# Two transformer layers in one program: feed forward's root on VectorE, layer 1's shifts by one product, two heads joined while leaving the bank, and a new table of ranks

## The chip, the core and the metric

The kernel runs on one core of one Trainium2 chip. The metric is the device time in microseconds (us) of one execution. PE is the matrix engine (TensorE), DVE is VectorE, ACT is ScalarE, POOL is GpSimd, and SP is the engine whose queue issues most DMAs. Each engine takes its instructions strictly in the order in which they were put into its queue, and waits at an instruction whose inputs are not there.

## The reference

Two layers over x of 4 batches x 512 tokens x 128 channels, 16 heads of 8 channels, windows of 64. Each layer adds attention times a gate:

```python
xn = layernorm(x)
s = L0_attn(xn)                 # masked window of 64 keys, 16 query and 4 value heads, fitness per head
g = silu(L0_ffn(xn))            # 8 experts; each token goes to one expert: gelu(x@w1+b1)@w2+b2, times 2
x = x + s * g
xn = layernorm(x)
s = L1_attn(xn)                 # below
g = silu(L1_ffn(xn))            # 8 experts, one per token: relu(x@w1+b1)@w2+b2
x = x + s * g

def L1_attn(h):
    y = layernorm(h, ln1)
    q, k, v = y @ wq + bq, y @ wk + bk, y @ wv + bv
    ctx = windows of 64 tokens, stepped by 32, softmax(q k^T / sqrt(8)) v,
          neighbouring windows blended with linear weights
    out = ctx @ wproj + bproj + h
    f = gelu(layernorm(out, ln2) @ w1 + b1) @ w2 + b2     # the feed forward
    return f + out
```

## The kernel before

**Tiles.** Attention of either layer goes through 16 tiles of 128 tokens (batch b, tile t). Each tile is a pipeline of steps: scores one way (s0, s1) only to get each query's largest score, then scores the other way (e0, e1) with the shift by that largest score added on PE, exp on ACT, the product with the values (ov0, ov1), a copy from the bank to SBUF (osb), PE transposes back to token order (o1), and the division by the row sum. Heads are kept as 4 groups (g) of 4 (j); in layer 1 a tile has two shifted sets of windows (par 0 and 1) and two blocks of 64 keys (w 0 and 1).

**Experts.** Both expert layers sort the 2048 tokens by expert into 23 blocks of 128 (`route`, from line 492). For every block POOL gathers its tokens (xb, line 609), SP fetches the weights (lines 615-630), PE does xt (a transpose), h and y, and POOL scatters the result to DRAM (yt, line 666). Each scatter follows the scatter before it. When all 23 are there, `gates` (line 672) loads the result back.

**Layer 1's shift** (in `queries1`, lines 1286-1303): DVE takes the maxima mx (L1290), `split` writes them as three bf16 terms into `shb` (L468-472), PE transposes `shb` (tr_sh), ACT copies it out (shd, L1298), and DVE multiplies it by four masks (sh4, L1301, 128 x 256 each). In `scores_k1` 16 products of 12 rows x 64 columns per tile add it to the scores.

**Layer 1's outputs** (`values1`, `outs1`): the two banks of a tile (w 0, 1) are copied whole, 128 x 512 each, by ACT or DVE, whichever the planner has free (`copied`, L344). PE transposes eight blocks of 128 x 128, a bank for each par; only the half of the columns that belongs to a head is read from them. DVE takes the reciprocals (L1380, once for each par), multiplies by the blend (L1382) and scales (L1386).

**Layer 1's feed forward** (`feed1`, eight halves named by batch and u, 0 or 2): pr (projection), sum and statistics on DVE, then 1/sqrt(variance + eps): DVE adds eps (`rsqrt`, L392) and POOL raises to the power -1/2 (L393). DVE normalizes (hn, L428), PE transposes (tr_hn), then f, gelu and fy. `rsqrt_many` (L395-408) is the same root by shifts and three Newton steps, 13 instructions on DVE; layer 0's queries and keys use it.

**What sets the order.** All steps are generators ("threads"). `run` (line 357) plays a small planner while the program is built: it keeps a time for PE (`now["T"]`), slots for DVE, ACT, POOL and SP, and takes next the thread that can start first; a tie goes to the smaller rank from the table at the end (one number for each thread and batch). `spent(cost, steps, events)` books a step: PE's cost times `pace()`, then the listed engine times. The order of each engine's queue comes from these booked times (`settle`). Where the planner sees PE waiting, `awake` puts products of ones of 128 x 512 in front of the next step (fillers), one for each 0.3 us.

Of the kernel before, what the change touches and what calls it, by code (L numbers as in the profile page):

```python
# [9 lines left out]
F32 = mybir.dt.float32  # L10
BF16 = mybir.dt.bfloat16
# [46 lines left out]
def two_layers(  # L58
# [43 lines left out]
    def bank(name):  # L102
        return awake(ps_m.tile([P, 512], F32, tag="m", name=name))
# [167 lines left out]
    def after(event):  # L271

        return None, max(0.0, at[event] - max(now["T"], now["-"]))
# [53 lines left out]
    def pace():  # L327
        return 1.8 if now["T"] < 70.0 else 1.12
# [66 lines left out]
    def rsqrt_many(dst, src, scale, eps):  # L395

        n = dst.shape[1]
        x = small.tile([P, n], F32, tag="rq_x", name=f"rq_x_{dst.tensor.name}", bufs=1)
        nc.vector.tensor_scalar(x, src, scale, eps, ALU.mult, ALU.add)
        y = small.tile([P, n], F32, tag="rq_y", name=f"rq_y_{dst.tensor.name}", bufs=1)  # L400
        nc.vector.tensor_single_scalar(y.bitcast(I32), x.bitcast(I32), 1, ALU.logical_shift_right)
        nc.vector.tensor_scalar(y.bitcast(I32), y.bitcast(I32), -1.0, float(0x5F3759DF), ALU.mult, ALU.add)
        nc.vector.tensor_scalar_mul(x, x, -0.5)
        z = small.tile([P, n], F32, tag="rq_z", name=f"rq_z_{dst.tensor.name}", bufs=1)
        for i in range(3):
            nc.vector.tensor_tensor(z, y, y, ALU.mult)
            nc.vector.tensor_tensor(z, z, x, ALU.mult)
            nc.vector.scalar_tensor_tensor(dst if i == 2 else y, z, 1.5, y, ALU.add, ALU.mult)
# [83 lines left out]
    def route(mask, n):  # L492
# [7 lines left out]
        with tc.high_priority():  # L500
# [53 lines left out]
            spent(0.35, [("D", 1.0)] * 7, [("rows", n)])  # L554
            in_places = []
            for q in range(2):
                in_place = att_p.tile([P, NTOK // 2, P], BF16, tag="osb0", name=f"in_place_{n}_{q}")
                i = q * NTOK // 2
                for u in range(NTOK // 2):
                    nc.vector.tensor_single_scalar(in_place[:, u], place_at, placef[:, i + u : i + u + 1], ALU.is_equal)  # L560
                in_places.append(in_place)
                spent(0, [after(("rows", n)), ("D", 1.2)], [("places", n, q)])
# [351 lines left out]
    shbs1 = prepared("shb1_", 2, [P, 2, G, 32], BF16)  # L914
    later.close()
# [288 lines left out]
    def project1():  # L1204

        for b in range(B):
            yield "-", [("xn1", b), ("s1", (b - 1) * NT - 1)]
# [30 lines left out]
    def queries1():  # L1238


        for i in range(NTILE):
# [52 lines left out]
            split(shb, mx, f"1_{b}_{t}")  # L1294
            spent(1.15, [("D", 2.45), ("D", 1.0)], [("s1", i), ("shb", i)], scores=1)
            yield "M", [("shb", i), ("e1", i - 2)]
            shd = att_p.tile([P, 2 * P], BF16, tag="shd1", name=f"shd1_{b}_{t}")
            nc.scalar.copy(shd, transposed16(shb.rearrange("p a g r -> p a (g r)"), 2, f"sh1_{b}_{t}"))  # L1298
            sh4 = att_p.tile([P, 2, J, P], BF16, tag="sh4_1", name=f"sh4_1_{b}_{t}")
            for j in range(J):  # L1300
                nc.vector.tensor_scalar_mul(sh4[:, :, j], shd.rearrange("p (a f) -> p a f", a=2), smask[:, j : j + 1])  # L1301
            asked1[i] = q4, sh4, v
            spent(0.13, [("A", 0.4), ("D", 1.2)], [("sh1", i)])

    def scores_k1():
        for i in range(NTILE):
# [9 lines left out]
            for par in range(2):  # L1316
# [8 lines left out]
                for w in range(2):  # L1325
                    for g in range(G):
                        r = slice(32 * g, 32 * g + NS * J)
                        mm(
                            ps[g // 2][w * KB : (w + 1) * KB, g % 2, par], ones16[r, 0:KB],
                            sh4[r, par, :, w * KB : (w + 1) * KB], start=False, stop=True,  # L1330
                        )
# [3 lines left out]
            spent(1.45, [("Ae", 1.03), ("Ae", 1.03)], [("e1", i)], scores=2)  # L1335

    def values1():
        for i in range(NTILE):
# [15 lines left out]
            osb = att_p.tile([P, 2, J, 2, KB], F32, tag="osb1", name=f"osb1_{b}_{t}", bufs=1)  # L1354
            ovs1[i] = osb
            for w, event in enumerate(("ov1", "ov1b")):
                copied(
                    osb[:, :, :, w].rearrange("p a j f -> p (a j) f"), ov[w].rearrange("p a c d f -> p (a c d) f"),
                    0.1 if w else 1.35, [(event, i)],
                )  # L1360

    def outs1():
        for i in range(NTILE):
# [4 lines left out]
            got = []  # L1368
            rec = small.tile([P, 2, 2, 2 * G], F32, tag="rec1", name=f"rec1_{b}_{t}")
            att = att_p.tile([P, 2, D], F32, tag="att1", name=f"att1_{b}_{t}", bufs=2)  # L1370
            for par in range(2):
                tp = bank(f"o1_{b}_{t}_{par}")
                for j in range(J):
                    turn(tp[:, j * P : (j + 1) * P], osb[:, par, j].rearrange("p w f -> p (w f)"), ident)

                tp = tp.rearrange("p (c h e) -> p c h e", c=2, e=32)
                skewed = [list(d) for d in tp.ap]
                skewed[1][0] += VC
                got.append(bass.AP(tensor=tp.tensor, offset=tp.offset, ap=skewed[0:3] + [[skewed[3][0], VC]]))
                nc.vector.reciprocal(rec[:, par], got[par][:, :, :, HD])  # L1380
                spent(0.5, [("D", 0.22)])
# [9 lines left out]
            spent(0, [("D", 0.85)], [("o1", i)], banks=2)  # L1391
# [21 lines left out]
    def feed1():  # L1413


        for b in range(B):
            for u in range(0, NT, 2):
# [16 lines left out]
                rsqrt(rs, mv[:, :, 1], LN_EPS)  # L1434
                centred(hn[:, two], res[:, two], mv, rs)
                spent(1.0, [("D", 0.7), ("D", 0.7), ("G", 1.0), ("D", 0.7)], [("pr", b, u)])
# [34 lines left out]
    def combine1():  # L1471
# [13 lines left out]
        (moe_h(0, gelu), 0, 59, 111, 16),  # L1485
        (scores_k1(), 87, 25, 32, 64),
        (project1(), 92, 81, 14, 102),
        (queries1(), 107, 26, 4, 78),
        (combine0(), 19, 20, 21, 22),
        (moe_load(0, xd0, w1_0, C_B1_0), 109, 42, 85, 68),  # L1490
        (moe_load_2(0, w2_0, b2_0), 18, 74, 23, 2),
        (gates(0, yt0), 56, 5, 6, 8),
        (values1(), 66, 112, 86, 55),
        (prepare0(), 31, 65, 95, 50),
        (moe_load(1, xd1, w1_1, C_B1_1), 35, 84, 34, 38),
        (moe_load_2(1, w2_1, b2_1), 101, 118, 37, 44),
        (scores_q(), 70, 36, 104, 94),
        (moe_x(0), 73, 93, 43, 96),
        (contexts1(), 11, 12, 54, 13),
        (project0(), 88, 106, 63, 62),  # L1500
        (moe_y(0, yt0), 117, 82, 90, 41),
        (moe_x(1), 67, 40, 46, 72),
        (gates(1, yt1), 103, 49, 114, 10),
        (values0(), 48, 15, 115, 124),
        (scores_k(), 33, 1, 58, 97),
        (route(mask0, 0), 45, 100, 24, 76),
        (fitness0(), 79, 61, 91, 69),
        (combine1(), 29, 30, 39, 99),
        (route(mask1, 1), 51, 83, 9, 75),
        (moe_y(1, yt1), 121, 71, 113, 127),  # L1510
        (outs0(), 47, 57, 125, 119),
        (masked0(), 7, 52, 53, 17),
        (moe_h(1, relu), 60, 3, 122, 105),
        (prepare1(), 27, 108, 28, 80),
        (outs1(), 120, 110, 116, 89),
        (feed1(), 126, 98, 123, 77),
# [45 lines left out]
```

## Time and profile before

| | us |
|---|---|
| median of 4 runs | 494.67 |
| lowest, highest | 493.94, 497.28 |
| the profiled execution's own time | 495.05 |
| span of its profile | 493.4 |
| mean granted TensorE clock | 0.925 of full speed |

The span runs from the first to the last recorded piece of work; the profiled execution's own time is 1.65 us longer. "Busy" is the time in which an engine had an instruction in work. In the groups, a line reads: source line, engine, operation, output<-input, partitions x elements, count, then busy time, mean length of one in ns, and the engine's idle time before them with what ended it. In the waits: who waited for whom, us in total, times, the longest. In the timeline: start, length, engine, line, operation, and in brackets the engine's idle time just before.

### The profile page before, as it was taken

The numbers are of one execution on the slowest core, as the hardware profiler recorded it, in microseconds if no ns is written. First come the engines' busy times: TensorE is split into PE (matmuls) and PEld (weight loads), VectorE is DVE, ScalarE is ACT, GpSimd is POOL, SyncE is SP. The second block draws the span as 40 slices with busy tenths as digits, with TensorE's granted clock in tenths as the row PEclk, the third lists the DMA queues.
The fourth block names the chain that finished last, engine by engine and source line by source line (L and its number), as shares of the span: only waits on it lengthen the run. The fifth ranks groups of instructions, "written<-read, shape, count | busy, mean of one in ns | idle before, by whom it ended". The sixth has DMA issues, their size and how long they took to land.

```text
span 493.4 us, 14720 instructions
## 1 busy us (share of the span) xinstructions
PE 414.8 (84%) x5663; PEld 293.1 (59%) x5663; DVE 339.4 (69%) x1013; ACT 261.3 (53%) x513; POOL 178.8 (36%) x251
## 2 busy tenths in 40 slices
PE   5877797999798687599999896878999993789985
PEld 2643564676565452355565574646879883678863
DVE  6799998553856978858774584884676660675565
ACT  1422665798477534374645655444666452346622
POOL 5751445536432222242410304136352336632311
PEclk9687699999999977679999998998999998799999
DMA  5404454867243010200000000061453673442032
GB/s 171 130 1 129 119 148 108 223 155 201 52 116 96 12 54 23 64 1 3 3 23 3 3 1 23 2 153 27 131 151 94 188 205 93 126 116 76 19 107 65
DMA packets 61894, 42.12 MB, mean 85 GB/s; under 512 B 11328, under 2 KB 54208, under 8 KB 61824
## 3 DMA queue, kind: packets, MB, share of 16 engines
q1 hardware_dynamic: 58464, 34.85, 25.7%
q0 software_dynamic: 2944, 6.04, 4.7%
q8 instruction: 45, 0.74, 0.6%
q10 hardware_dynamic: 416, 0.29, 0.2%
q14 instruction: 25, 0.20, 0.1%
HBM read 34.99 MB, written 6.16 MB: 83 GB/s over the span
## 4 chain that ended last, share of the span: by engine, by line
PE 47%; DVE 27%; issue 9%; ACT 6%; DMA 5%; POOL 4%; SPq 1%; POOLq 0%; ACTq 0%; DVEq 0%
PE e L83 8%; PE s L83 6%; PE h L83 5%; PE y L83 4%; PE ov L83 4%; DVE mx L1009 3%; DVE mx L1290 3%; PE fy L83 3%; PE f L83 2%; PE qkv L83 2%; DMA xb<-xd,tokens_at 2%; ACT th L1017 2%; DMA wb<-in_w 1%; PE v L83 1%; DVE sm L1009 1%
## 5 line engine op out<-in xcount | busy, mean ns | idle before, releaser
L666 POOL DMA_INDIRECT yt<-yb,put_at x46 | 46.1, 1002 | 103.4 <-DMA yt<-yb,put_at 18.5
L609 POOL DMA_INDIRECT xb<-xd,tokens_at x46 | 45.3, 984 | 51.5 <-DVE tokens_at L586 17.1
L83 PE MATMUL h<-xbT,wb 128*128 128x128 f32 x368 | 51.4, 292 | 2.2 <-ACT xbT L344 1.3
L83 PE MATMUL y<-wb,hb 128*128 128x128 f32 x368 | 49.3, 283 | 3.5 <-ACT hb L696 3.2
L83 PEld LDWEIGHTS h<-xbT,wb 128*128 128x128 f32 x368 | 46.6, 203 | 8.5 <-issue 3.3
L83 PEld LDWEIGHTS y<-wb,hb 128*128 128x128 f32 x368 | 45.6, 197 | 7.0 <-ACT hb L696 3.9
L83 PE MATMUL e<-q,kd 32*64 32x256 f32 (+1 forms) x864 | 43.7, 444 | 0.4 <-ACT pt L1106 0.4
L1017 ACT ACTIVATE th<-s 128x768 f32<-128x768 f32 x32 | 26.0, 813 | 29.7 <-DVE mx L1009 29.1
L1333 ACT ACTIVATE pt<-e 128x1024 f32<-128x1024 f32 x32 | 31.0, 1021 | 19.7 <-PE e L83 19.7
L1290 DVE TENSOR_REDUCE mx<-s 128x16 f32<-128x1024 f32 x32 | 37.6, 1218 | 4.7 <-PE s L83 4.6
L83 PE MATMUL s<-k,qd 32*32 32x384 f32 (+1 forms) x1024 | 37.2, 484 | 2.6 <-ACT pt L1333 2.3
L83 PEld LDWEIGHTS <-ones 12*64 12x64 bf16 (+2 forms) x439 | 21.4, 105 | 28.1 <-issue 20.0
L1106 ACT ACTIVATE pt<-e 128x1024 f32<-128x1024 f32 x32 | 31.0, 1021 | 13.0 <-PE e L83 13.0
L1009 DVE TENSOR_REDUCE mx<-s 128x8 f32<-128x768 f32 x32 | 29.3, 950 | 11.8 <-PE s L83 11.8
L344 ACT COPY osb<-ov 128x512 f32<-128x512 f32 x33 | 18.5, 587 | 27.1 <-PE ov L83 21.7
L696 ACT ACTIVATE hb<-h,bb 128x128 f32<-128x128 f32 x92 | 26.4, 381 | 10.4 <-PE h L83 9.8
L1009 DVE TENSOR_REDUCE sm<-th 128x8 f32<-128x768 f32 x32 | 30.0, 948 | 1.3 <-ACT th L1017 1.0
L83 PE MATMUL ov<-pt,va 64*32 64x128 f32 (+1 forms) x896 | 28.9, 290 | 0.4 <-DVE ctx L344 0.2
L83 PEld LDWEIGHTS e<-q,kd 32*64 32x64 f32 x864 | 19.0, 136 | 11.2 <-issue 6.0
L1251 POOL TENSOR_TENSOR q<-qd,jmask 128x640 f32<-128x640 f32 x16 | 19.9, 1257 | 14.8 <-PE e L83 13.5
L704 ACT ACTIVATE hb<-h,bb 128x128 f32<-128x128 f32 x56 | 15.8, 375 | 14.5 <-PE h L83 11.9
L83 PE MATMUL e<-sh,ones 12*64 12x256 bf16 (+1 forms) x320 | 20.5, 305 | 3.6 <-DVE sh L1301 3.6
(287 smaller groups left out, 899.3 us busy)
## 6 DMA issues: line engine op xcount, KB each, us to landing
wb<-in_w SPq DMA_DIRECT2D x92, 256.0 KB
bb<-in_b SPq DMA_DIRECT2D x46, 64.0 KB
acc<-yt SPq DMA_DIRECT2D x8, 256.0 KB
xd<-ln_a SPq DMA_DIRECT2D x4, 256.0 KB
xd<-xr SPq DMA_DIRECT2D x4, 256.0 KB
out<-acc SPq DMA_DIRECT2D x8, 128.0 KB
x<-in_x SPq DMA_DIRECT2D x3, 256.0 KB
bb<-in_cols SPq DMA_DIRECT2D x46, 2.0 KB
```

Source lines behind the costliest of these rows:

```text
L83: ins = nc.tensor.matmul(*args, **kw)
L344: (nc.scalar.copy if e == "A" else nc.vector.tensor_copy)(dst, src)
L609: nc.gpsimd.indirect_dma_start(out=xb, out_offset=None, in_=xd, in_offset=bass.IndirectOffsetOnAxis(ap=tokens_at[:, k : k + 1], axis=0),)
L666: nc.gpsimd.indirect_dma_start(out=yt, out_offset=bass.IndirectOffsetOnAxis(ap=routed[n][0][:, k : k + 1], axis=0), in_=y, in_offset=None,)
L696: nc.scalar.activation(h[:, c, :], src[:, c * P : (c + 1) * P], AF.Gelu, bias=bias[:, c : c + 1])
L704: nc.scalar.activation(dst, src_c, AF.Relu, bias=b)
L1009: nc.vector.tensor_reduce(dst[:, t, 8 * gg : 8 * gg + 8].rearrange("p (u j) -> p u j", u=2), src.rearrange("p u (j f) -> p u j f", j=J), A ...
L1017: nc.scalar.activation(th, ps[gg], AF.Tanh, scale=0.5 * SCALE)
L1106: nc.scalar.activation(pt[:, 2 * gg : 2 * gg + 2], ps[gg], AF.Exp)
L1251: engine.tensor_tensor(dst, src[:, None, o : o + TW].to_broadcast([P, J, TW]), jmask[:, :, None].to_broadcast([P, J, TW]), ALU.mult,)
L1290: nc.vector.tensor_reduce(mx.rearrange("p a g j -> p g a j")[:, 2 * gg : 2 * gg + 2], ps[gg], AX.X, ALU.max, negate=True,)
L1333: nc.scalar.activation(pt[:, 2 * gg : 2 * gg + 2], ps[gg], AF.Exp, scale=SCALE)
```

## The change

1. `feed1` calls `rsqrt_many` instead of `rsqrt`: POOL's power is gone, and 13 small DVE instructions of two columns take its place. `rsqrt_many` takes one size of scratch tile for all its callers.
2. Layer 1's shift: `split` writes a compact tile (`terms`), and one DVE product with a mask (`own`) writes it into `shb` once for each of the two key blocks. Two products with `fold` (128 x 64) take the place of the two transposes; ACT's copy and the four mask products have half the columns. In `scores_k1` 8 products of 32 rows x 128 columns (`lane`) take the place of 16.
3. Layer 1's outputs: each bank leaves by one ACT instruction (two heads, scaled by `pick`) and one DVE instruction that adds the other two. `osb` has half the size and two buffers. Four transposes instead of eight, in one bank, and one reciprocal.
4. Five small constants (`own`, `fold`, `lane`, `smask1`, `pick`) are made by ten DVE instructions.
5. The planner's numbers: `pace` is 1.45 and 1.08 for 1.8 and 1.12, the routing's DVE steps are booked shorter, and all 128 ranks are others. So most steps of both layers stand elsewhere in every queue.

```diff
     def pace():
-        return 1.8 if now["T"] < 70.0 else 1.12
+        return 1.45 if now["T"] < 70.0 else 1.08
...
-            spent(0.35, [("D", 1.0)] * 7, [("rows", n)])
+            spent(0.35, [("D", 0.47)] * 7, [("rows", n)])
...
+            if b == 0:
+                yield "-", [("mask", 0)]
+                half = small.tile([P, 2, 2], F32, tag="half", name="half", bufs=1)
+                nc.vector.tensor_reduce(half[:, 0], ident.rearrange("p (w q) -> p w q", w=2), AX.X, ALU.add)
+                nc.vector.tensor_copy(own, half[:, 0])
+                nc.vector.tensor_tensor(fold, ident16[:, 0:KB], ident16[:, KB:P], ALU.add)
...
             shb = shbs1[i % 2]
-            split(shb, mx, f"1_{b}_{t}")
+            terms = small.tile([P, 2, G, NS * J], BF16, tag="terms", name=f"terms_{b}_{t}", bufs=1)
+            split(terms, mx, f"1_{b}_{t}")
+            nc.vector.tensor_tensor(
+                shb.rearrange("p a g (c r) -> p (a g) c r", c=2)[:, :, :, 0 : NS * J],
+                terms.rearrange("p a g r -> p (a g) r")[:, :, None].to_broadcast([P, 2 * G, 2, NS * J]),
+                own[:, None, :, None].to_broadcast([P, 2 * G, 2, NS * J]), ALU.mult,
+            )
...
-            shd = att_p.tile([P, 2 * P], BF16, tag="shd1", name=f"shd1_{b}_{t}")
-            nc.scalar.copy(shd, transposed16(shb.rearrange("p a g r -> p a (g r)"), 2, f"sh1_{b}_{t}"))
-            sh4 = att_p.tile([P, 2, J, P], BF16, tag="sh4_1", name=f"sh4_1_{b}_{t}")
+            for par in range(2):
+                mm(ps[:, par], shb[:, par].rearrange("p g r -> p (g r)"), fold, start=True, stop=True)
+            nc.scalar.copy(shd, ps)
+            sh4 = att_p.tile([P, 2, J, KB], BF16, tag="sh4_1", name=f"sh4_1_{b}_{t}")
...
-                for w in range(2):
-                    for g in range(G):
-                        r = slice(32 * g, 32 * g + NS * J)
-                        mm(
-                            ps[g // 2][w * KB : (w + 1) * KB, g % 2, par], ones16[r, 0:KB],
-                            sh4[r, par, :, w * KB : (w + 1) * KB], start=False, stop=True,
-                        )
+                for g in range(G):
+                    r = slice(32 * g, 32 * g + 32)
+                    mm(ps[g // 2][:, g % 2, par], lane[r], sh4[r, par], start=False, stop=True)
...
             for w, event in enumerate(("ov1", "ov1b")):
-                copied(
-                    osb[:, :, :, w].rearrange("p a j f -> p (a j) f"), ov[w].rearrange("p a c d f -> p (a c d) f"),
-                    0.1 if w else 1.35, [(event, i)],
+                nc.scalar.activation(osb[:, :, :, w], ov[w][:, :, 0], AF.Copy, scale=pick[:, 0:1])
+                nc.vector.scalar_tensor_tensor(
+                    osb[:, :, :, w], ov[w][:, :, 1], pick[:, 1:2], osb[:, :, :, w], ALU.mult, ALU.add
                 )
...
-                for j in range(J):
-                    turn(tp[:, j * P : (j + 1) * P], osb[:, par, j].rearrange("p w f -> p (w f)"), ident)
+                for d in range(2):
+                    o = (2 * par + d) * P
+                    turn(tp[:, o : o + P], osb[:, par, d].rearrange("p w f -> p (w f)"), ident)
...
-                rsqrt(rs, mv[:, :, 1], LN_EPS)
+                rsqrt_many(rs, mv[:, :, 1], 1.0, LN_EPS)
                 centred(hn[:, two], res[:, two], mv, rs)
-                spent(1.0, [("D", 0.7), ("D", 0.7), ("G", 1.0), ("D", 0.7)], [("pr", b, u)])
+                spent(1.0, [("D", 0.7), ("D", 0.75), ("D", 0.75), ("D", 0.75)], [("pr", b, u)])
...
-        (moe_h(0, gelu), 0, 59, 111, 16),
-        (scores_k1(), 87, 25, 32, 64),
+        (moe_h(0, gelu), 72, 107, 99, 117),
+        (scores_k1(), 13, 11, 102, 80),
...
```

## The prediction

> **What bounds the kernel now.** I read the page first, for each engine's share and its course over time.
>
> ```profile
> span 493.4 us, 14720 instructions
> PE 414.8 (84%) x5663; PEld 293.1 (59%) x5663; DVE 339.4 (69%) x1013; ACT 261.3 (53%) x513; POOL 178.8 (36%) x251
> PE   5877797999798687599999896878999993789985
> DVE  6799998553856978858774584884676660675565
> ```
>
> PE is the bound in most slices. DVE is it in the first fifth: between 23 and 75 us it is busy for 49.6 of 52. PE has 78.6 us of idle time, so next I asked the waits which of it is long.
>
> ```profile
> PE tr_hn L88 <- DVE hn L428: 12.5, 3, 10.4
> DVE hn L428 <- POOL rs_d L393: 20.6, 8, 13.3
> POOL yt L666 <- DMA yt<-yb,put_at: 18.5, 6, 4.1
> ```
>
> One wait of 10.4 us stands out, of PE on the feed forward's hn, and DVE's wait on POOL's power behind it is longer still (13.3). The timeline shows its place:
>
> ```profile
> 407.38 0.16 DVE L392 TENSOR_SCALAR rs_d<-mv_d 128x2 f32<-128x2 f32 x1
> ...
> 416.21 1.00 POOL L666 DMA_INDIRECT yt<-yb,put_at  x1 [0.17 <-issue]
> 417.51 0.97 POOL L609 DMA_INDIRECT xb<-xd,tokens_at  x1 [0.30 <-issue]
> 418.79 0.96 POOL L609 DMA_INDIRECT xb<-xd,tokens_at  x1 [0.30 <-DMA yt<-yb,put_at]
> 420.05 1.00 POOL L666 DMA_INDIRECT yt<-yb,put_at  x1 [0.30 <-issue]
> 421.08 0.73 POOL L393 TENSOR_TENSOR rs_d<-rs_d,neghalf 128x2 f32<-128x2 f32 x1
> 421.85 0.60 DVE L428 TENSOR_SCALAR hn<-xr,mv_d,rs_d 128x128 f32<-128x128 f32 x2 [13.26 <-POOL rs_d L393]
> 422.34 0.66 PE L88 MATMUL tr_hn<-ident,hn 128*128 128x128 f32 x2 [10.45 <-DVE hn L428]
> ```
>
> The variance is ready at 407.5. POOL reaches a power of 0.73 us at 421, since scatters and gathers of the second expert layer stand ahead of it. Everything behind hn on DVE and behind tr_hn on PE stands still.
>
> **Root by VectorE (8 halves).** Away: POOL's power (0.74 each) and that stall. The root then ends by 407.5 + 13 x 0.19 = 410.0 (0.19 is the distance of dependent one-column instructions in the startup, 9.07 to 9.26 to 9.45), hn by 410.6, while PE is busy until 411.9. So 10.4 us go. I take all of it; the other end is 0, if another POOL wait takes its place. Added: 13 dependent instructions, 2.5 us, for 0.17 + 0.1 + 0.74 + 0.05 = 1.1 us through POOL. In the last two halves nothing covers this: +1.4 each, counted in the tail. The other six lie beside experts and attention. DVE's load grows by 8 x (13 x 0.06 to 13 x 0.2), 6 to 21 us. (The Trainium skill, "VectorE: DVE Perf Modes", section on the trn2 errata, speaks against such a chain: a fixed cost for each instruction, about 150 cycles measured, whatever its size. By it I estimate 13 x 0.156 = 2.0 us for each root, 16 us in all. The trace's independent one-column instructions last 0.15 but follow each other every 0.06 us; the chain here is dependent, so its 0.19 stands nearer to the page.)
>
> **Shift by one product (16 tiles).** Less: the four mask products have 128 instead of 256 columns: L1301 is busy 15.8 us for 64, the 128-wide L560 5.5 for 32, so 64 x (0.247 - 0.172) = -4.8. More: one DVE product of 192 columns, between L471 (32 columns, 0.20) and L1431 (256, 0.42), taken as 0.3, 16 x 0.3 = +4.8. In the chain from mx to exp it is +0.3 - 0.3 - 0.1 (ACT's copy), nothing. On PE, 16 small products become 8: in the e1 tile at 377.07 the first eight cost 0.11 us until the next group starts and the last eight 0.36; four of 512 columns in layer 0's tile at 252.91 cost 0.33 until the next, so half that twice, 0.33 for 0.47: -0.1 a tile, -1.6 us; range -4 to +2. (The skill's "TensorEngine Tiling (Array Packing)", Key Properties, says that a change of tiling mode drains the engine, and that different tiles work in parallel. Both speak against this edit: eight 32x64 tiles already ran side by side, and 32x128 is a new mode four times a tile. Layer 0 makes the same switch at 252.91, 0.07 us before the products ahead of it end; no drain is to be seen, so I charge none.)
>
> **Two heads joined (16 tiles).** The rows:
>
> ```profile
> L88 PE MATMUL o<-ident,osb 128*128 128x128 f32 x128 | 17.7, 283 | 0.6 <-ACT osb L344 0.6
> L344 ACT COPY osb<-ov 128x512 f32<-128x512 f32 x33 | 18.5, 587 | 27.1 <-PE ov L83 21.7 <-issue 2.3 <-PE xt L88 1.3
> L344 DVE COPY osb<-ov 128x512 f32<-128x512 f32 x15 | 10.3, 689 | 13.5 <-PE ov L83 13.5
> L1380 DVE RECIPROCAL rec<-o 128x16 f32<-128x16 f32 x32 | 7.6, 247 | 12.7 <-PE o L88 12.3
> ```
>
> Eight transposes take 0.88 us of PE (376.27, 0.87), four take 0.44: 16 x 0.44 = -7.0, 15 of these tiles ahead of the tail, -6.6, in stretches where PE is 85 to 97% busy. Taken whole; at worst half. Eviction: now ACT 0.38 (as ctx, 128x256) and then DVE 0.42 for each bank, against one copy of 0.59 or 0.69. Two banks take 0.4 + 0.4 + 0.43 = 1.2 instead of 0.6 to 1.2; hidden behind the next steps on PE, and 0.6 on the last tile. DVE: 32 x 0.42 = 13.4 for some 9 copies (6.2), and half the reciprocals (-3.6): +3.6.
>
> **Constants.** The new kernel's DVE queue has seven of the ten ahead of the first off (L766): five reductions like L840 and L842 (0.2 to 0.28) and two small ones: 1.4 us. At 9.91 off ran straight behind such constants, and ACT had waited 5.4 us for it. So +1.4 on the path.
>
> **DVE's load** grows by about 6 to 25 us in all, on an engine that is 69% busy. Its lag behind PE costs 0 to 6; taken as +2.
>
> **The order.** I followed PE's and DVE's queues of the new kernel.
> First route: it now stands behind the second batch's norm (7.7 us of DVE) and the reductions of one more tile (4 x 0.93). tokens_at moves from 46.4 to about 57.5, and h of block 0 from 54.5 to 65. But DVE was full either way and has these things done. Where the first e0 tile starts (85.2 before), the new order has one s0 tile more and one h less behind it, and I get 89: +3.5, taken as +2.5 beyond the constants; range 0 to +11.
> Layer boundary: at the last y of the first experts (174.9), batch 3's projections and some outputs (5 us of PE) are left; they fall into the 23 us in which PE waited for layer 1 (17.6 busy): -4, range 0 to -8.
> Second experts: they begin some two attention tiles earlier, so more is left to fill them.
> Tail: s1, sh, e1 of the last tile and ov1 of the one before (1.05 + 0.2 + 1.39 + 1.1 = 3.7) now stand behind the last y; f and fy of half 2 of batch 2, two c and tr_hn (2 + 2 + 0.7) come before it: +1.0 ahead of it. Behind it the last tile runs uncovered: s1 to maxima 3.55, split and product 1.15, fold, copy and masks 1.4, shift 0.5, exp with its table 3.4, ov 1.15; beside it pr and the DVE root (to 13.2), hn, tr_hn, hT and f (to 16.8); then o and the division 1.6, c and its copy 0.8, fy 1.4 more: pr of the last half at 20.6. From that pr to the end it was 14.0 (479.4 to 493.4), plus 1.4: 36.0 from the last y, where it was 31.8 (461.6 to 493.4).
> Fillers: 149 instead of 119, 20 more ahead of the tail, 0.25 each (tokens: 20 take 4.5). They go where the planner sees PE waiting; half counted, +2.5.
>
> **The sum.** The last y ends at 461.6 + 1.0 (moved) - 10.4 (stall) - 6.6 (transposes) - 1.5 (shift, 15 tiles) + 1.4 (constants) + 2.5 (first route) - 4 (boundary) + 2.5 (fillers) + 2 (DVE) = 448.5. With 36.0 the span is 484.5. The profiled execution took 1.65 more than its span and 0.4 more than the median (495.05, 494.67): 484.5 + 1.65 - 0.4 = 485.8, rounded to 486.
>
> **Rivals.**
> A, slower: the late first route is not made good. From 80 to 125 us PE is 94 to 98% busy, so 11 us lost there stay lost, and with the experts' end at 186 the boundary has nothing to gain: 486 + 8.5 + 4 = 498.5. It decides from the point where the last y of the first experts ends some 8 us later than 174.9. For it: PE's full slices. Against: DVE, not PE, held 23 to 75.
> B, no change: POOL's lag stays and another step waits for it, since each scatter still follows the one before (18.5 us of such waits) and q for e1 (L1251) stands behind scatters too. The stall is only moved: 486 + 10.4 = 496.4, or 493 with part of it. For it: POOL was three scatters late at 407. Against: in the new POOL queue q and the gathers stand 12 to 25 us of PE work ahead of their users.
> C, faster still: the fillers fall into real waits, DVE does not lag and the boundary gives 8: 486 - 2.5 - 2 - 4 = 477.5. That the shift's edit saves nothing on PE is +1.5 inside my range.
>
> **How the numbers follow.** About 0.5% (2.5 us) is what a measurement of this kernel can tell from no change: faster is below 492.2, slower above 497.1. My case with C holds 0.72, all of it faster; A 0.19, slower; B 0.09, no change. The time is that of my case, 486. The range leaves out the lower half of C (0.07) and the upper part of A (0.12): 477.5 to 499. The likeliest case alone is 478 to 492.
>
> **What would show it.** Right: no wait of tr_hn above 2 us outside the last two halves; eight roots of 2 to 3 us on DVE; o at half its busy time; the last y near 448 and 35 to 37 us behind it; h of the first block near 65 and the last y of the first experts near 174. Wrong: a wait of 5 us or more on POOL's q or xb between 320 and 450; a DVE busy share above 80% in the second layer with PE waiting for mx or sh; the first experts' last y past 183.

## The result, and the profile after

The changed kernel took 523.47 us (median of 22 runs, 519.58 to 528.3), the kernel before 495.3 beside it (32 runs): ratio **1.056, interval 1.054 to 1.059**. It is slower by 28 us; the forecast was 486. (Disturbed runs are left out of the ratios; of the joined heads' four runs below that leaves two.) The profiled execution took 525.43 us, its span 523.7 at a mean clock of 0.896; before it was 493.4 at 0.925.

The same rows as in the prediction, from the page of the kernel after, and PE's granted clock:

```profile
span 523.7 us, 14511 instructions
PE 430.7 (82%) x5501; PEld 290.7 (56%) x5501; DVE 366.1 (70%) x1134; ACT 261.2 (50%) x528; POOL 175.6 (34%) x243
PE   5972787899899957778899688699799998799595
DVE  6689889624896867587765877576776666755843
PEclk8586898899999978858779999899899998989978
```

PEclk of the page before:

```profile
PEclk9687699999999977679999998998999998799999
```

PE has 162 fewer instructions and is busy 15.9 us longer. The reason stands in the clock. By the mean clocks 74 us before (2 x (1 - 0.925) x 493.4) and 109 after are granted at half speed. Laid over PE's busy times, the trace's clock steps give 54.7 us of busy time at half speed before and 91.3 after, so half of the difference, 18.3, is the same work done slower, if half the clock doubles its time. Idle time grew by 14.4 (78.6 to 93.0). The work itself, at full speed, shrank by 2.4: 14.4 + 18.3 - 2.4 = the 30.3 us between the spans. This is bookkeeping, and no cause yet.

The waits of PE after (us in total, times, the longest):

```profile
PE s L83 <- ACT th L1024: 16.6, 8, 6.9
PE tr_hn L88 <- DVE hn L428: 15.0, 6, 4.2
PE sh L83 <- DVE shb L1320: 14.2, 8, 4.2
PE tr_k L88 <- DVE qk L963: 8.9, 3, 6.2
```

The one stall of 10.4 us on POOL's power is gone, and no wait of PE in this list is on POOL. The three tiles of DVE in it cost PE 38.1 us in 17 waits; the same three (hn, the shift's shb, qk) cost 22.7 in 13 before, the stall among them. The wait of s on ACT's th grew from 6.5 to 16.6.

Four points of the course, in us:

| | before | forecast | after |
|---|---|---|---|
| last y of the first experts ends | 174.9 | 174 | 171.4 |
| tokens of layer 1 end | 325.3 | - | 327.3 |
| last y of the second experts ends | 461.6 | 448.5 | 480.8 |
| from there to the end of the span | 31.8 | 36.0 | 42.9 |

Up to the last y of the first experts the forecast held. It fell in three places: the beginning of layer 1's attention, the second experts, the tail. Windows of 30 us at that beginning, of before and then of after (the window, PE, PEld, DVE, ACT and POOL busy with their instructions, PEclk, DMA share, GB/s):

```profile
205.00:235.00 30.00, 28.91 (x397) 16.43 (x403) 20.73 (x55) 17.08 (x32) 9.77 (x12) 0.84 0.04 11
235.00:265.00 30.00, 28.58 (x596) 17.20 (x582) 20.82 (x67) 16.29 (x27) 7.42 (x6) 1.00 0.04 11
```

```profile
205.00:235.00 30.00, 23.28 (x238) 12.68 (x240) 21.58 (x45) 11.62 (x24) 7.67 (x9) 0.70 0.04 10
235.00:265.00 30.00, 25.88 (x398) 13.56 (x390) 21.53 (x60) 12.16 (x20) 6.87 (x6) 0.78 0.01 2
```

Over these 60 us together (a product that crosses 235 stands in both rows) PE did 980 products before and 628 after. Its waits there come to 2.3 us before and 13.5 after, and each of them names ACT or DVE. What was not done there is done later: of the products of attention (s, e, ov) 1264 before and 1468 after lie behind the tokens of layer 1, and 64 and 193 behind the last y of the second experts.

### The profile page after: what moved, and what is told of

Its sections match the earlier page's. It is cut to its first block, busy times and chain, and to the rows that moved or that the text cites. A ratio compares the mean times of both kernels' runs of the same rounds, so it can differ in the third digit from the quotient of the medians.

```text
span 523.7 us, 14511 instructions
## 1 busy us (share of the span) xinstructions
PE 430.7 (82%) x5501; PEld 290.7 (56%) x5501; DVE 366.1 (70%) x1134; ACT 261.2 (50%) x528; POOL 175.6 (34%) x243
## 4 chain that ended last, share of the span: by engine, by line
PE 49%; DVE 35%; ACT 8%; issue 4%; DMA 2%; POOL 1%; SPq 0%; ACTq 0%; DVEq 0%; POOLq 0%
PE e L83 10%; DVE mx L1314 6%; PE s L83 6%; PE y L83 5%; PE h L83 5%; PE ov L83 3%; ACT th L1024 3%; PE f L83 3%; PE fy L83 3%; DVE mx L1016 2%; DVE sm L1016 2%; PE lg L83 2%; PE o L88 1%; PE v L83 1%; PE qkv L83 1%
## 5 line engine op out<-in xcount | busy, mean ns | idle before, releaser
L83 PE MATMUL h<-xbT,wb 128*128 128x128 f32 x368 | 49.2, 282 | 4.4 <-DVE xbT L344 4.2
L83 PEld LDWEIGHTS h<-xbT,wb 128*128 128x128 f32 x368 | 45.0, 195 | 7.9 <-DVE xbT L344 4.4
L83 PE MATMUL e<-q,kd 32*64 32x256 f32 (+1 forms) x864 | 46.4, 475 | 0.2 <-DVE mx L1314 0.2
L83 PE MATMUL s<-k,qd 32*64 32x256 f32 (+1 forms) x1024 | 40.4, 511 | 2.9 <-ACT th L1024 1.6
L1363 ACT ACTIVATE pt<-e 128x1024 f32<-128x1024 f32 x32 | 31.0, 1021 | 22.7 <-PE e L83 22.7
L1275 POOL TENSOR_TENSOR q<-qd,jmask 128x640 f32<-128x640 f32 x16 | 21.0, 1325 | 50.2 <-ACT qd L1257 25.4
L83 PEld LDWEIGHTS <-ones 128*128 128x128 bf16 (+1 forms) x213 | 17.6, 108 | 28.7 <-issue 21.5
L696 ACT ACTIVATE hb<-h,bb 128x128 f32<-128x128 f32 x92 | 26.2, 385 | 4.8 <-PE h L83 4.6
L83 PEld LDWEIGHTS e<-q,kd 32*64 32x64 f32 x864 | 16.9, 142 | 13.0 <-issue 8.2
L704 ACT ACTIVATE hb<-h,bb 128x128 f32<-128x128 f32 x64 | 18.2, 375 | 11.1 <-PE h L83 6.1
L1076 POOL TENSOR_TENSOR q<-q2d,wmask 128x512 f32<-128x512 f32 x16 | 17.1, 1074 | 19.7 <-PE e L83 17.2
L1388 ACT ACTIVATE osb<-ov,pick 128x256 f32<-128x256 f32 x32 | 13.5, 470 | 19.3 <-PE ov L83 19.2
```

Of the source, the lines that this page charges most:

```text
L83: ins = nc.tensor.matmul(*args, **kw)
L696: nc.scalar.activation(h[:, c, :], src[:, c * P : (c + 1) * P], AF.Gelu, bias=bias[:, c : c + 1])
L704: nc.scalar.activation(dst, src_c, AF.Relu, bias=b)
L1076: nc.gpsimd.tensor_tensor(q4, q2s[b][:, None, f].to_broadcast([P, J, P]), wmask[:, :, None].to_broadcast([P, J, P]), ALU.mult)
L1275: engine.tensor_tensor(dst, src[:, None, o : o + TW].to_broadcast([P, J, TW]), jmask[:, :, None].to_broadcast([P, J, TW]), ALU.mult,)
L1363: nc.scalar.activation(pt[:, 2 * gg : 2 * gg + 2], ps[gg], AF.Exp, scale=SCALE)
```

## The experiments

Two theories. **Order**: the ranks, paces and booked costs, and every edit through its bookings, make the planner lay out another order of PE's work, and that order is worse. **Edits**: the operations themselves cost more than the prediction's rows said. The runs fell on several chips. On some the kernel before takes 495 us, on others 507, so only ratios to the kernel before on the same chip are compared, and traces only with a trace from a chip of like speed.

### The planner's numbers alone, and the edits alone

e1_numbers is the kernel before with 32 new lines of ranks, the paces 1.45 and 1.08 and the route's new costs; e2_code is the kernel after with the old ones.

```
-        return 1.8 if now["T"] < 70.0 else 1.12
+        return 1.45 if now["T"] < 70.0 else 1.08
-        (moe_h(0, gelu), 0, 59, 111, 16),
+        (moe_h(0, gelu), 72, 107, 99, 117),
...
```

> The kernel before, with only the planner's numbers of the change in it: the 32 lines of ranks, the two paces and the costs booked for the route's steps; no operation of the kernel is edited. Theory N (the new order makes the loss: the layer boundary is left with gaps on PE, whose granted clock then falls to 0.7, and the last tile stands uncovered behind the last y): 510 to 525 us, with the windows 206 to 266 at a clock below 0.85 and a tail over 38 us. Theory E (the edited operations make it: four changes of tiling a tile, a longer chain of DVE from mx to exp, two engines for each eviction, 13 dependent instructions a root): 492 to 500, with a clock of 0.95 there. If both have a share, between the two.

> The kernel after, with only the planner's numbers of before in it (ranks, paces and the costs booked for the route's steps), so all edits in nearly the old order. Theory N (order): 485 to 497, at or below the kernel before, since the edits then bring what the prediction counted for them. Theory E (edits): 510 to 525, with the waits of PE on shb, hn and qk as in the kernel after, and a low clock at the layer boundary all the same.

Measured: e1 524.73 against 506.76, **1.034** (1.024 to 1.043); e2 520.03, **1.028** (1.017 to 1.039). Neither theory has it alone, and the two multiplied, 1.063, are near the whole. Without any edit the new order makes the hole at the start of layer 1. Windows of e1_numbers:

```profile
205.00:235.00 30.00, 24.00 (x242) 14.84 (x236) 18.97 (x45) 15.73 (x30) 7.76 (x9) 0.78 0.06 18
235.00:265.00 30.00, 24.95 (x363) 13.48 (x357) 20.48 (x47) 10.74 (x18) 4.38 (x4) 0.72 0.01 2
```

That is 591 products in the 60 us. The chip is a slower one; on such a chip k0_control (the program of the kernel before, further down) has 874, and e2_code, with the old numbers, 814 at a clock of 0.89 and 1.00. Later stages of these traces, in us:

| | tokens of layer 1 to the last y of the second experts | from there to the end |
|---|---|---|
| kernel before | 136.3 | 31.8 |
| kernel after | 153.5 | 42.9 |
| kernel before on a slower chip (k0_control) | 146.9 | 32.6 |
| e1_numbers | 164.8 | 30.6 |
| e2_code | 149.4 | 43.1 |

So the new order alone makes the loss beside the second experts, and not the long tail that was expected of it (over 38); the long tail comes with the edits or the order that they draw. (With the order held, below, they make it 38.8 for 32.6.) Ranks, paces and booked costs were not tried apart.

### Is the half clock the cause there?

e8_fill is the kernel after with 48 more products with ones in that stretch, two ahead of each half of a score tile.

```
     def banks(name):
+        if 205.0 < now["T"] < 262.0:
+            now["gap"] = max(now["gap"], 0.61)
         awake(ps[:, 0])
```

> The kernel after with 48 more of the products with ones (512 columns, 0.22 us each, 10.4 us of PE at full clock), two ahead of each score tile that the planner places between 205 and 262 us, where PE ran at a clock of 0.75 and was idle 11 us of 57; nothing is booked for them. If the half clock there is a cause (theory S): the clock of that stretch rises above 0.9, layer 1's attention runs earlier by 5 to 12 us, and the ratio to the kernel before falls from 1.056 to 1.03 to 1.05. If the half clock is only a sign of a chain through ACT and DVE that sets the pace: no change or up to 10 us slower (1.056 to 1.075).

Measured: 526.11 against 495.81, **1.064** (1.056 to 1.072). The clock rose (in the two windows from 0.70 and 0.78 to 0.84 and 0.94, over 205 to 325 from 0.84 to 0.90), and the router's last product of layer 1 came 107.1 us behind its first instead of 105.7: nothing gained. At this place the half clock is a sign more than a cause. That the chain through ACT and DVE between one tile and the next sets the pace is what PE's waits there name; the run itself doesn't single it out, since its own products take PE's time too. So the 18.3 us of the bookkeeping may not be taken as a loss that a better clock would give back.

### Two edits taken back in the new order

e3_lane64 adds the shift by 64 columns of lane at a time, with all bookings as they were; e4_pool_root gives the root back to POOL and books it so:

```
-                for g in range(G):
-                    r = slice(32 * g, 32 * g + 32)
-                    mm(ps[g // 2][:, g % 2, par], lane[r], sh4[r, par], start=False, stop=True)
+                for w in range(2):
+                    for g in range(G):
+                        r, k = slice(32 * g, 32 * g + 32), slice(w * KB, (w + 1) * KB)
+                        mm(ps[g // 2][k, g % 2, par], lane[r, k], sh4[r, par], start=False, stop=True)
```

```
-                rsqrt_many(rs, mv[:, :, 1], 1.0, LN_EPS)
+                rsqrt(rs, mv[:, :, 1], LN_EPS)
```

> The kernel after, with each shift added by sixteen products of 32 rows by 64 columns of lane instead of eight of 32 by 128; order, bookings and everything else stay. So the e1 tile keeps one tiling throughout. If the change of tiling drains PE and that is on the path: e1's time on PE falls from 1.68 to about 1.45 a tile, 16 x 0.23 = 3.7 us at full clock, and 4 to 8 us of the total with what waits behind it. If the 1.68 is hidden by other waits: no difference within 1.5 us of the kernel after.

> The kernel after, with the feed forward's root of layer 1 by POOL's power again (booked as before the change). If the removal of POOL's stall is worth what the prediction took for it, this is 5 to 12 us slower than the kernel after (528 to 535), with a wait of PE on hn over 5 us. If the 13 dependent DVE instructions cost as much as the stall, it is within 3 us of it, and if they make a part of the loss (they lasted 3.9 us where POOL worked beside them, and stand in the tail twice), it is 3 to 8 us faster (515 to 520).

Measured: e3 544.65 against 506.76, 1.072 (1.062 to 1.082); e4 544.05, 1.073 (1.061 to 1.084). PE's time of an e1 tile did fall in e3, as this shows. From the kernel after, an e1 tile and the transpose behind it (start, us, engine, line, operation):

```profile
419.88 0.69 PE L83 MATMUL e<-q,kd 32*64 32x256 f32 x16
420.50 0.29 PE L83 MATMUL e<-sh,lane 32*128 32x256 bf16 x4
420.72 0.69 PE L83 MATMUL e<-q,kd 32*64 32x256 f32 x16
421.34 0.29 PE L83 MATMUL e<-sh,lane 32*128 32x256 bf16 x4
421.56 0.66 PE L88 MATMUL o<-ident,osb 128*128 128x128 f32 x4
```

From e3_lane64:

```profile
401.36 0.69 PE L83 MATMUL e<-q,kd 32*64 32x256 f32 x16
401.85 0.31 PE L83 MATMUL e<-sh,lane 32*64 32x256 bf16 x8
401.95 0.77 PE L83 MATMUL e<-q,kd 32*64 32x256 f32 x16
402.39 0.45 PE L83 MATMUL e<-sh,lane 32*64 32x256 bf16 x8
402.77 0.23 PE L83 MATMUL sh<-fold,shb 128*128 128x64 bf16 x2
```

The tile takes 1.68 us (419.88 to 421.56) with four changes of tiling and 1.41 without; 1.39 is the usual value of the kernel before and of e3. In the total no gain can be read: the only ratio to set beside e3's is the kernel after's 1.056, from faster chips. Nor does e4 price the root. Its booking makes the planner draw PE's order anew; against e3 its tail is 15.0 us shorter (28.7 for 43.7), and its second experts end 12.5 us later (514.5 for 502.0).

### One edit at a time on the old ranks

e5_root has only the root of the kernel before changed, e6_join only the joined heads, e7_shift only the shift. Each diff is the part of the change that the name says, and the planner orders freely.

> The kernel before with one edit of the change: layer 1's feed forward takes its root by 13 instructions of VectorE, ranks and all else as before (the planner moves steps where the new booking makes it). By the prediction: the stall of 10.4 us goes, 1.4 us twice come into the tail, DVE's lag gives back 0 to 2: ratio 0.975 to 0.985. Theory S (removed waits are paid back by scattered shorter ones, each of which throws PE to half its clock for at least one further step of 3.41 us): 0.99 to 1.01, with at least as many half-clock steps as before and PE waits on hn in several halves instead of one.

> The kernel before with one edit: two heads joined on the way out of the bank (half the transposes and reciprocals, ACT and then VectorE for each bank). By the prediction: 6.6 us of PE less, 3.6 of DVE more: ratio 0.985 to 0.995. If the two engines in a row make it later on the path (0.47 and 0.48 us a bank, as the kernel after shows, and DVE's queue ahead of it): 1.00 to 1.015, with PE waiting for osb or the bank.

> The kernel before with one edit: layer 1's shift by the product with fold, 64-wide copies, and eight products with lane a tile. By the prediction: -1.6 us of PE and nothing in the chain: ratio 0.995 to 1.00. By the e1 tile's 1.68 us for 1.39 (16 x 0.29 = 4.6 us) and the DVE product of 0.41 us in the chain from the maxima to the exponential: 1.01 to 1.025. The kernel with all three edits in this order was at 1.028, so the three ratios should multiply to that.

Measured, all against 495.81: e5 **1.028** (1.019 to 1.036), e6 **1.033** (1.021 to 1.045), e7 **1.043** (1.034 to 1.053). Each alone costs as much as all three together in e2. That can't be a sum of costs of operations. In e5's trace the stall is gone and the second experts end as early as before (last y at 460.5), but from there to the end it takes 48.0 us instead of 31.8.

### An order that moves with nothing edited

```
-        return 1.8 if now["T"] < 70.0 else 1.12
+        return 1.8 if now["T"] < 70.0 else 1.13
```

> The kernel before with one number of the planner changed: the pace that it reckons with behind 70 us is 1.13 instead of 1.12. No operation, no tile and no rank is changed; the planner's order of PE moves about as far as by one of the edits. Theory O: 1.01 to 1.04, a loss like that of the single edits, with nothing edited. Theory E: 0.99 to 1.01.

Measured: 513.52 against 506.39, **1.014** (1.006 to 1.021). A hundredth in one pace costs 7 us, and every free redraw tried here loses.

### The edits with PE's order held

Here the planner's picks are replayed from the kernel before, and its products with ones too:

```
+        picks = iter(PICKS)
...
+            pick = ids[id(extra[0])] if extra else "ABC...".index(next(picks))
             for i, (g, ranks, (k, needs)) in enumerate(asked):
+                if ids[id(g)] != pick:
+                    continue
...
-        n, now["gap"] = max(0, int(now["gap"] / 0.3)), 0.0
+        n, now["gap"] = FILLS.get(name, 0), 0.0
```

> The kernel before, its planner's choices replayed from the list: the same program, instruction for instruction. Ratio 1.00, which shows the noise of these comparisons, and a profile of the old kernel from the chip that runs the others of this call. If PE's stall on hn is about 10 us again, the root's edit with PE's order held lost its gain elsewhere; if it is below 5 us, the stall of the profile that the prediction read is not the one that most runs have.

> The kernel before with the root by VectorE alone, and PE's order held: the planner's choices are replayed from the kernel before, one by one, and so are its products with ones, so that PE's sequence is the same instruction for instruction; only the queues of the other engines move where the new steps are booked. Theory O (each edit makes the planner draw another order, and an order that was not chosen for this code costs some 3%, whatever the edit): 0.975 to 0.995, as the prediction has it for the root, where the same edit in the free order was 1.028. Theory E (the root itself costs it, by DVE's load and lag): 1.02 to 1.035, as in the free order.

> The kernel before with two heads joined on the way out of the bank, and PE's order held in the same way (half the transposes are gone, everything else stands in the same sequence). Theory O: 0.985 to 1.00 (1.033 in the free order). Theory E (two engines in a row for each eviction): 1.02 to 1.04.

> The kernel before with the shift by one product, and PE's order held in the same way. Theory O: 1.00 to 1.015, the 16 x 0.29 us of the changed tiling and the DVE product being left (1.043 in the free order). Theory E (the longer chain from the maxima to the exponential, and the tiling): 1.03 to 1.045.

> All the edits of the change on the old ranks, paces and costs, with PE's order held as in the kernel before. Theory O (order): what the three single edits cost with the order held, multiplied: 1.003 x 1.012 x 1.012 = 1.027 at most, and down to 1.01 if the joined transposes pay beside the others. If the edits hinder one another (all three load DVE), more than 1.03. The prediction's own sum without its terms for the order: 0.97.

Measured: k0 1.001 (0.997 to 1.006); root 1.003 (0.997 to 1.009); shift **1.012** (1.007 to 1.018); all edits **1.032** (1.020 to 1.044). Joined heads: four runs, 503.4, 507.0, 518.2 and 519.4, against 506.4; they lie too far apart for an interval, and no difference can be told. So the root's 2.8% and 3 of the shift's 4.3% were the order's; how much of the joined heads' 3.3% was stays open. All three together cost about the same with the order held (1.032) as in the free order (1.028), so this part of the loss is not the order of PE, which was the same product for product but for those that the edits themselves take away or put in. The shift's 1.2% is in it. Whether the rest is the joined heads or something that the edits do to one another, all three being work for DVE, is not shown: the single ratios multiply to 1.015 without the joined heads and, by the record's estimate, to 1.027 with them, which the interval includes.

### The root once more: where the stall's 10 us went

e14_root6_kept leaves POOL's root in the last two halves:

```
-                rsqrt(rs, mv[:, :, 1], LN_EPS)
+                rsqrt_many(rs, mv[:, :, 1], 1.0, LN_EPS) if b < B - 1 else rsqrt(rs, mv[:, :, 1], LN_EPS)
```

> The kernel before with the root by VectorE in the first six halves and by POOL in the last two, PE's order held. If the two roots of the tail give back what the stall's removal brought (the last y to the end took 37.9 us with them, 32 to 34 in the other runs with the order held): 0.99, 4 to 5 us less than with all eight. If the gain is lost in the stretch after the stall: 1.00, as with all eight.

> The same kernel as e9_root_kept (all eight roots by VectorE, PE's order held). If the kernel before runs in some 495 us on this chip (a chip on which the stall of 10 us shows): 10.4 less the stall, 2.8 to 5 more in the tail, ratio 0.985 to 0.995. If it runs in some 506 us: 1.00, as before.

> The same kernel as e14_root6_kept (POOL's root kept in the last two halves). At 495 us for the kernel before: 0.975 to 0.985, the whole stall without the price in the tail. At 506 us: 0.99 to 1.00 again, 4 to 5 us below the one with all eight.

Measured: e14 **0.994** (0.990 to 0.998) on a chip of 509 us. On one of 496: e16, all eight roots, **1.000** (0.995 to 1.005); e17, six roots, **0.988** (0.984 to 0.992), 489.74 against 495.88. e14 and e17 beat the kernel before, and e16 and e17 can be read beside the kernel before, stage by stage, since PE's sequence is the same and the speed of the chip alike. The waits of PE between 325 and 465 us before, and then between 325 and 460 in e16:

```profile
PE tr_hn L88 <- DVE hn L428: 10.4, 1, 10.4
PE tr_sh L88 <- DVE shb L472: 3.2, 5, 0.9
PE xt L88 <- DMA xb<-xd,tokens_at: 1.7, 1, 1.7
```

```profile
PE xt L88 <- DMA xb<-xd,tokens_at: 5.0, 4, 1.5
PE e L83 <- POOL q L1256: 2.9, 1, 2.9
PE tr_sh L88 <- DVE shb L477: 2.3, 3, 1.3
```

The stall is gone; 2.9 us come back as a wait on POOL's q and 3.3 more on the gathers. From the first h to the last y of the second experts it takes 121.7 us instead of 126.8: the stall's removal is worth 5 us, not 10.4 (6 in e17, with 120.7). It is worth as much where no such stall shows: e14 takes 130.0 us there, k0_control on the same chip 136.4. These are single executions, which differ by some 3 us. In the tail e16 takes 38.8 us, e17 32.1, before 31.8. This is the first of the two halves in e16:

```profile
465.37 1.46 PE L83 MATMUL tr_hn<-ones 128*128 128x512 bf16 x6
...
466.88 0.16 DVE L411 TENSOR_TENSOR rq_z_rs_d<-rq_y_rs_d 128x2 f32<-128x2 f32 x1
467.09 0.63 ACT L687 ACTIVATE tg<-acc 128x512 f32<-128x512 f32 x1 [4.58 <-DMA acc<-yt]
467.75 0.69 DVE L688 SCALAR_TENSOR_TENSOR acc<-tg,acc 128x512 f32<-128x512 f32 x1 [0.71 <-ACT tg L687]
468.36 0.15 DVE L412 TENSOR_TENSOR rq_z_rs_d<-rq_z_rs_d,rq_x_rs_d 128x2 f32<-128x2 f32 x1
468.48 0.42 DVE L1482 SCALAR_TENSOR_TENSOR acc<-acc,xr 128x256 f32<-128x256 f32 x1
468.82 0.15 DVE L413 SCALAR_TENSOR_TENSOR rq_y_rs_d<-rq_z_rs_d,rq_y_rs_d 128x2 f32<-128x2 f32 x1
...
471.21 0.73 PE L88 MATMUL tr_hn<-ident,hn 128*128 128x128 f32 x2 [4.39 <-DVE hn L433]
...
472.60 3.78 PE L83 MATMUL f<-hT,fw_sb 128*128 128x256 f32 x8
```

The same f in e17:

```profile
466.91 1.99 PE L83 MATMUL f<-hT,fw_sb 128*128 128x256 f32 x8 [0.22 <-ACT hT L1451]
```

Between the fifth and the sixth instruction of the root stands an accumulation of the output, which waits for ACT, which waited for the experts' result to be loaded back; one more lies between each of the next four pairs. The root takes 4.7 us (466.09 to 470.77) instead of the 2.3 of the other half. From pr's end to tr_hn it is 6.55 us in e16 and 3.80 with POOL in e17, where POOL's power runs beside all that. PE stands idle for 4.4 instead of 1.6, and the clock falls behind it: over the tail it is 0.91 in e16 and 1.00 in e17 (0.97 before), and f takes 3.78 us instead of 1.99.

### The same in the tail of the new order

e15_after_root6 is the kernel after, its own order held, with the last two roots by POOL (the same line as in e14).

> The kernel after, its own order held, with the root of the last two halves by POOL. In it PE waits for hn 3.7 and 2.1 us in the tail, and behind both at half clock. By POOL the root is a chain of 1.1 us for 2.5 or more: 2.8 us off by the prediction's price, 4 to 6 with the clock, so 1.045 to 1.052 for 1.056.

Measured: 538.66 against 509.29, 1.064 (1.055 to 1.073): no gain to be seen beside 1.056, which comes from faster chips. e3_lane64 stands on a chip of like speed and has nearly the same order of PE: its tail takes 43.7 us, e15's 35.9, and its second experts end at 502.0, e15's at 499.2. So the two roots cost the tail some 8 us in this order too, and the second experts' end 18 us behind the kernel after's goes with the slower chip.

## Why the prediction was wrong, step by step

The prediction's terms, in us, beside what the runs with PE's order held and e1_numbers give:

| | forecast | measured |
|---|---|---|
| the stall | -10.4 | -5 to -6 (e16, e17) |
| two roots in the tail | +2.8 | +7 (e16 against e17) |
| the shift | -1.5 | +6.3 (e11) |
| the joined heads | -6.6 | no difference can be told (e10) |
| all edits, with constants (+1.4) and DVE's lag (+2) | -12.3 | +16 (e12) |
| the new order | +3.4 | +17 (e1) |

So both halves failed: the edits' own terms by some 28 us, the order's by some 14.

**The order, +3.4.** The prediction read the two queues for what stands where and charged the new order with single pieces: first route +2.5, boundary -4, moved work +1.0, fillers +2.5, and the uncovered last tile in the tail (4.2 with the roots' 2.8 in it). Up to the last y of the first experts this held (174 forecast, 171.4). For layer 1 it assumed that an order which keeps all work also keeps PE as full as before; the second experts, with more left to fill them, got no price. e1_numbers shows 3.4% for the order alone, and its traces show where: 591 products instead of k0_control's 874 in the first 60 us of layer 1's attention, and 164.8 us instead of 146.9 from the tokens to the last y of the second experts. None of the rivals had this; the sign for A (first experts past 183) and the DVE share did not come.

**The stall, -10.4.** PE's wait of 10.4 us is gone, but 5 to 6 us are left of it with PE's order held. This is rival B's mechanism in part: POOL's q and the gathers come next (2.9 and 3.3 us). The stall was also less fixed than it looked. DVE's hn waits for POOL's power in other kernels that keep it, 10.6 us in e6_join and 8.8 in e7_shift, but PE then had other work in its own order and waited 2.3 and 1.6 at most; in e10_join_kept PE waits 7.5, and in k0_control, the same program on a slower chip, 1.3. One profiled execution's longest wait was taken as the program's. Nor did the sign of no wait of tr_hn above 2 us outside the last two halves come: the longest there is 4.2 in the kernel after.

**The roots of the tail, +1.4 each.** Measured +7.0 for two (38.8 for 31.8; 6.7 against e17). The price of 13 x 0.19 = 2.5 was right for an undisturbed root (2.3 us). What was missed is that DVE serves other work between the instructions and, being in order, waits with it, 2.7 us from pr to tr_hn, and that the clock then falls on what follows. The sign of eight roots of 2 to 3 us did not come either: in the kernel after they take 2.3 to 6.9 us, six of them over 3.5. In the longest two single instructions of two columns last 1.21 us each while POOL is at work on q; why was not tried.

**The shift, -0.1 a tile.** Measured +0.29 a tile (1.68 for 1.39), 4.6 us in all, and 6.3 us of the total with PE's order held (1.2% of 506.4). Here the prediction named the rule that speaks against the edit, the Trainium skill's "TensorEngine Tiling (Array Packing)", Key Properties: a change of tiling mode drains the engine. It set it aside for a place in layer 0 where it saw no drain, and there it misread the trace: it looked at the products, which follow 0.07 us before those ahead of them end, in layer 0 (252.91) as in the new tile (420.50). The gap stands in the weight loads. First layer 0's in the kernel before, then lane's in the kernel after:

```profile
252.91 0.10 PEld L83 LDWEIGHTS <-ones 12*128 12x128 bf16 x4 [0.39 <-issue]
```

```profile
420.49 0.10 PEld L83 LDWEIGHTS <-lane 32*128 32x128 bf16 x4 [0.39 <-issue]
```

Both come 0.39 us after the loads ahead of them, with no cause named. So the trace agrees with the page, and the tile is 0.29 longer, 0.07 for each of the four changes.

**The joined heads, -6.6.** The transposes were halved (o: 12.1 us busy for 64 products, 17.7 before for 128, since each lasts longer, 0.32 for 0.28), but no gain in time can be told with the order held. The evictions cost more than assumed:

```profile
L88 PE MATMUL o<-ident,osb 128*128 128x128 f32 x64 | 12.1, 321 | 0.0
L1389 DVE SCALAR_TENSOR_TENSOR osb<-ov,pick,osb 128x256 f32<-128x256 f32 x32 | 14.8, 479 | 4.1 <-ACT osb L1388 3.9
L1388 ACT ACTIVATE osb<-ov,pick 128x256 f32<-128x256 f32 x32 | 13.5, 470 | 19.3 <-PE ov L83 19.2
L1320 DVE TENSOR_TENSOR shb<-terms,own 128x192 bf16<-128x192 bf16 x16 | 6.5, 407 | 0.3
L1416 DVE RECIPROCAL rec<-o 128x32 f32<-128x32 f32 x16 | 5.7, 356 | 21.7 <-PE o L88 21.5
```

That is 0.48 and 0.47 us a bank where 0.42 and 0.38 were taken from plain copies, 0.41 for the shift's product, taken as 0.3, and reciprocals at three quarters of their former busy time (7.6), not half.

**DVE's lag, +2.** DVE grew by 26.7 us, just over the range given (6 to 25; its terms add up to 10 to 25), and PE's waits on its three tiles grew by 15.4 us, though the stall of 10.4 left them. The share stayed at 70%; the load told nothing, the place of the load did.

**Constants and route** came near the forecast: first h at 62.7 (65), first e0 at 93.9 (89), and the first experts made it good. The constants are eight DVE instructions, not ten, and the first off starts 0.7 us later (10.61 for 9.91), not 1.4.

What stays open: why the new order starves PE at the start of layer 1 tile by tile, what the joined heads cost, and whether the three edits hinder one another on DVE or merely add up.

## What to carry to other kernels

An order drawn by a planner belongs to the code and the costs that it was drawn for: a hundredth in one pace cost 1.4%, and an edit that is judged in a freshly drawn order is judged with that draw. Hold the order fixed, replaying it if a planner makes it, before an edit is priced or thrown away; here a root that looked 2.8% slower cost nothing, and gained 1.2% in six of its eight places. A chain of many small instructions is priced by what else its in-order engine has queued between them, not by its own length: it fits where other work covers it, not in the tail.

## What the runs showed of the hardware

**The clock and gaps.** In the two traces (before and after) the clock changes only at the ends of steps of 3.41 us. All 28 falls to half came behind a step in which PE was busy for at most 0.58 of the time, and none of the 212 other steps at full clock was below 0.44: the border lies near half. Full speed returned only behind a step that was at least 0.86 busy, and not behind each of those. So a gap of 1.6 us can halve the clock for 3.41 more, while the stall of 10.4 us in the kernel before had 4.1 us at half clock behind it. The Trainium skill's "TensorE: Matmul & The Clock Gate", Part 1, gives the window as 3413 ns, which the lengths of these steps agree with; it speaks of idle gaps of over 3.4 us, and here gaps of half that length, such as the 1.57 us from 221.2 ahead of the half clock from 223.6 in the kernel after, were among those that it followed.

**The same program on two chips.** The program of the kernel before takes some 495 us on some chips; as k0_control it took 508 on another. Behind 325 us k0_control's trace has 14 places where a product of attention started 0.55 us or more after the product before it with nothing named as the cause. The other traces from chips of its speed have 3 to 15 of them; those from the faster chips, e16 and e17 with PE's sequence unchanged among them, have none. One e1 tile of it:

```profile
374.46 0.30 PE L83 MATMUL e<-sh,ones 12*64 12x256 bf16 x2 [0.33 <-issue]
375.21 0.33 PE L83 MATMUL e<-sh,ones 12*64 12x256 bf16 x3 [0.45 <-issue]
376.67 0.37 PE L83 MATMUL e<-sh,ones 12*64 12x256 bf16 x1 [1.13 <-issue]
```

This tile took 4.18 us, part of it at half clock, instead of 1.39. What starves PE there was not tried.
